# Four fused layers on one core: in the first (retention) layer, |scores| of two quads are added on GpSimd for half of the heads before they are summed on TensorE

## The chip, the core and the metric

One core of a Trainium2 chip. The whole program (four layers, one launch) runs on it, and the metric is the device time of one execution in microseconds. The engines are named as in the profile: PE (TensorE), PEld (its weight loads), ACT (ScalarE), DVE (VectorE), POOL (GpSimd), SP (SyncE, which here only issues DMAs).

## The reference, cut to what matters

The input is 8 images of 32x32 positions and 256 channels. Four layers follow one another, each added to its input. The change touches only the first, a retention layer with 8 heads of 32 channels and L = 1024 tokens:

```python
xf = groupnorm(x).reshape(B, L, E)
q, k, vr = heads(xf @ Wq.T), heads(xf @ Wk.T * SCALING), heads(xf @ Wv.T)
qr, kr = theta_shift(q, sin, cos), theta_shift(k, sin, cos)     # q*cos + rot(q)*sin
qk  = einsum('bhqd,bhkd->bhqk', qr, kr) * mask[None]
den = clip(abs(qk).sum(-1, keepdims=True), 1.0, 50000.0)
out = einsum('bhqk,bhkd->bhqd', qk / den, vr)
out = layernorm_over_head(out) * ln_g + ln_b
out = gelu(out) @ Wo.T
```

So each score is needed twice: as it is (for `out`) and as an absolute value summed over the keys (for `den`).

## The kernel before, in words

**Quads.** `layer0` cuts the work of an image into 32 *quads* (L655 on): for each half `c` of the heads (4 heads), each half `h` of the 1024 queries, and each of 8 blocks `kb` of 128 keys. All 8 images make 256 quads, numbered n. A quad handles 4 heads at once, in two PSUM tiles `s` of 128 x (2 heads x 512 queries); the ring of `s` tiles has 3 places.

**What one quad does.**
- `scores(n)` (L668): for each of the two tiles, two 32-row matmuls on PE (L675; each fp32 matmul is two instructions in the profile, so a quad has eight), then DVE multiplies the tile with the decay mask into SBUF, `e` (L681).
- `absolute(n, i)` (L683): ACT writes `ea = |e|` (L685).
- `sums(n - 2)` (L687): four matmuls with a 128 x 32 block of ones add up `ea` over the keys into the PSUM tile `sm` (L693). This is "a set of sums"; every quad has one, for the quad two before it. After kb = 7, DVE clamps `sm` into `dn` (L701).
- `nums(n - 1)` (L709): four matmuls of `v` with `e` into `num` (L720); after kb = 7 ACT copies it to `nm` (L728).

The loop at the end of `layer0` emits, for each n: scores(n), absolute(n, 0), sums(n-2), nums(n-1), absolute(n, 1), and then the *units* that are due.

**Units.** All other work is cut into units and given to `fill` with the number of a quad, after which it is emitted: `project` (q or k of one half of the tokens: 2 matmuls L550, a DVE shuffle L554 into `sh`, an ACT copy L555 into `xc`; after the second half POOL rotates: L560, L561, L563 for k, and L565, L567 as well for q), `values` (L534, L538), `normed` (POOL writes the normalised image `xn`, L236), `gn.stats/mean/root` (the group norm's statistics on DVE, with two tiny matmuls and a `pow` on POOL, L223), `ahead` (SP loads a coming image), and for each half of the heads the `tail`: POOL makes `sq` = nm*nm + dn*dn*1e-5 (L578, L579, with an ACT Square L576), `var` (L584, then a table load, Ln and Exp on ACT), `norm` (two DVE multiplies of `sq` and `nm`, L591, then a table load and Gelu on ACT), and `output` (L603, a DVE add L608, a store by SP).

**Order.** PE, DVE and ACT run in the order in which `layer0` writes the instructions (`manual_schedule`); on POOL and SP the order is a scheduler's. Each engine runs its queue in order. PE needs `e` from DVE for nums, `ea` from ACT for sums, and a free `s` place for scores and for every unit's PSUM tile (they share the ring).

**Memory.** `x` images and the next layer's first tiles share a ring of three 1 MB buffers, `K.big`; `xn` has its own buffer; `ea` has 4 buffers, `e` 4.

Of the kernel before, what the change touches and what calls it, by code (L numbers as in the profile page):

```python
# [434 lines left out]

class Fillers:


# [20 lines left out]
def layer0(tc, K, src, dst, n_img, a, first):  # L461
    nc = tc.nc
    with tc.tile_pool(name="l0c", bufs=1) as cp, tc.tile_pool(
# [48 lines left out]
        def flat(t):  # L512
            return t.rearrange("p a n -> p (a n)")

        xn, v, qk, hT, nm, dn, turned = ({} for _ in range(7))
        fill = Fillers()

        K.ring = lambda name: pair(name)[:, 0, :]
        gn = GroupNorm(K, n_img)

        def normed(b):
            gn.shift(b)
            xn[b] = wk.tile([P, 2, L], F32, name="xn")
            for c in range(2):
                gn.apply(nc.gpsimd, b, c, xn[b][:, c, :], x[b][:, c, :])

        def values(b, u):
            if u == 0:
# [13 lines left out]
        def project(b, s, c, h):  # L542
            if h == 0:
                turned[0] = wk.tile([P, L], F32, name="sh")
                turned[1] = wk.tile([P, L], F32, name="xc")
            sh, xc = turned[0], turned[1]
            ps = pair("qk_ps")[:, 0]
            hs = slice(h * HALF, (h + 1) * HALF)
            for kc in range(2):
                nc.tensor.matmul(  # L550
                    ps, w[:, s, kc, c * P : (c + 1) * P], xn[b][:, kc, hs],
                    start=kc == 0, stop=kc == 1,
                )
            nc.vector.stream_shuffle(sh[:, hs], ps, [i ^ 1 for i in range(32)])  # L554
            nc.scalar.copy(xc[:, hs], ps)  # L555
            if h == 0:
                return
            d = wk.tile([P, L], F32, name=f"qk{s}{c}")
            qk[b, s, c] = d
            nc.gpsimd.tensor_mul(v3(sh), v3(sh), hankel(63))  # L560
            nc.gpsimd.tensor_mul(v3(xc), v3(xc), hankel(0))  # L561
            if s == 1:
                nc.gpsimd.tensor_add(d, xc, sh)  # L563
            else:
                nc.gpsimd.tensor_add(xc, xc, sh)  # L565
                o = 126 + 32 * c
                nc.gpsimd.tensor_mul(  # L567
                    v3(d), v3(xc), rot[:, o : o + 32].unsqueeze(2).to_broadcast([P, 32, 32])
                )


        def tail(b, c):
            m, d = nm.pop((b, c)), dn.pop((b, c))
            if c == 0:
                hT[b] = wk.tile([P, 2, L], F32, name="hT")
            nc.scalar.activation(d, d, AF.Square, scale=math.sqrt(1e-5))  # L576
            sq = wk.tile([P, L], F32, name="sq")
            nc.gpsimd.tensor_mul(sq, flat(m), flat(m))  # L578
            nc.gpsimd.tensor_add(sq, sq, flat(d))  # L579

            def var():
                ps = pair("var_ps")
                for h, hs in halves():
                    nc.tensor.matmul(ps[:, h], hd[:, 1, :], sq[:, hs], start=True, stop=True)  # L584
                nc.scalar.preload_act_table_set("natural_log_exp_and_others")
                nc.scalar.activation(sq, flat(ps), AF.Ln)
                nc.scalar.activation(sq, sq, AF.Exp, scale=-0.5)

            def norm(h):
                hs = slice(h * HALF, (h + 1) * HALF)  # L590
                nc.vector.tensor_mul(sq[:, hs], m[:, h], sq[:, hs])  # L591
                if h == 1:
                    nc.scalar.activation(
                        hT[b][:, c, :], sq, AF.Gelu, bias=gb[:, 1:2], scale=gb[:, 0:1]
                    )

            return var, norm

        def output(b, m, h):
            ps = pair("o_ps")[:, 0]  # L600
# [13 lines left out]
        def prepare(b):  # L614

            n = 32 * b
            for i in range(4):
                fill.add(
                    n + (0, 1, 3, 4)[i],
                    lambda s=1 - i // 2, h=i % 2: project(b, s, 1, h),  # L620
                )
            if b == 0 and n_img > 1:
                x[1] = load(1)
                measure(1, 6)
            if b + 2 < n_img:
                def ahead():
                    x[b + 2] = load(b + 2)

                fill.add(n + 16, ahead)
                measure(b + 2, n + 23)  # L630
            if b + 1 < n_img:
                fill.add(n + 15, lambda: normed(b + 1))
                for i in range(4):
                    fill.add(
                        n + (17, 18, 20, 21)[i],
                        lambda s=1 - i // 2, h=i % 2: project(b + 1, s, 0, h),
                    )
                    fill.add(n + 23 + i, lambda u=i: values(b + 1, u))

        def measure(b, at):  # L640
            for i in range(4):
                fill.add(at + i, lambda i=i: gn.stats(b, image_parts(x[b]), i))
            fill.add(at + 5, lambda: gn.mean(b))
            fill.add(at + 7, lambda: gn.root(b))

        def follow(nx):
            n = 32 * n_img
            for i, u in enumerate(nx.early()):
                fill.add(2 + i if i else 0, u)
            fill.add(n - 46, nx.load)  # L650
            for i in range(4):
                fill.add(n - 38 + i, lambda i=i: nx.stats(i))
            fill.add(n - 33, nx.mean)
            fill.add(n - 31, nx.root)
            for c in range(2):  # L655
                fill.add(n - 27 + c, lambda c=c: nx.norm(c))
            fill.add(n - 12, nx.weights)

        quads = [
            (b, c, h, kb)  # L660
# [4 lines left out]
        ]  # L665
        e, ea, acc = {}, {}, {}

        def scores(n):  # L668
            b, c, h, kb = quads[n]
            o = (28 - 4 * kb) * 32 + HALF * h  # L670
            for i in range(2):
                s = pair("s")
                for j in (2 * i, 2 * i + 1):
                    g = slice(32 * j, 32 * j + 32)
                    nc.tensor.matmul(  # L675
                        s[:, j % 2], qk[b, 1, c][g, kb * P : (kb + 1) * P],
                        qk[b, 0, c][g, h * HALF : (h + 1) * HALF], start=True, stop=True,
                    )
                e[n, i] = wk.tile([P, 2, HALF], F32, name="e", bufs=4)
                m = mask[:, 4 * c + 2 * i : 4 * c + 2 * i + 2, o : o + HALF]  # L680
                nc.vector.tensor_mul(e[n, i], s, m)  # L681

        def absolute(n, i):  # L683
            ea[n, i] = wk.tile([P, 2, HALF], F32, name="ea", bufs=4)
            nc.scalar.activation(ea[n, i], e[n, i], AF.Abs)  # L685

        def sums(n):  # L687
            b, c, h, kb = quads[n]
            if kb == 0:
                acc["sm"] = pp.tile([P, HALF], F32, tag="sm", name="sm")  # L690
            for j in range(4):
                g = slice(32 * j, 32 * j + 32)
                nc.tensor.matmul(  # L693
                    acc["sm"][g, :], ones, ea[n, j // 2][:, j % 2, :],
                    start=kb == 0, stop=kb == 7,
                )
            del ea[n, 0], ea[n, 1]
            if kb == 7:
                if h == 0:
                    dn[b, c] = wk.tile([P, 2, HALF], F32, name="dn")  # L700
                nc.vector.tensor_scalar(  # L701
                    dn[b, c][:, h], acc["sm"], 1.0, 50000.0, ALU.max, ALU.min
                )
                if h == 1:
                    var, norm = tail(b, c)
                    fill.add(n + 7, var)
                    for h in range(2):
                        fill.add(n + 9 + h, lambda h=h: norm(h))
                    if c == 1:  # L709
                        for i in range(4):  # L710
                            fill.add(n + 12 + i, lambda i=i: output(b, i // 2, i % 2))

        def nums(n):
            b, c, h, kb = quads[n]
# [15 lines left out]
        engines = {mybir.EngineType.PE, mybir.EngineType.DVE, mybir.EngineType.Activation}  # L730
        with tc.manual_schedule(engines=engines):
            gn.stats(0, image_parts(x[0]))
            gn.mean(0)
            gn.root(0)
            normed(0)
            for s in (1, 0):
                for h in range(2):
                    project(0, s, 0, h)
            for u in range(4):
                values(0, u)  # L740
            N = len(quads)
# [2 lines left out]
            for n in range(N + 2):  # L744
                if n % 32 == 0 and n < N:
                    prepare(n // 32)
                if n < N:
                    scores(n)
                    absolute(n, 0)
                if n >= 2:  # L750
                    sums(n - 2)
                if 1 <= n <= N:
                    nums(n - 1)
                if n < N:
# [1608 lines left out]
```

## Time and profile before

| | us |
|---|---|
| time, median of 3 runs | 3330.1 (3329.66 to 3331.37) |
| the profiled execution's own time | 3334.75 |
| its span, first to last instruction | 3333.0 |
| first quad's scores start | 40.0 |
| last quad's scores start | 1060.9 |
| first matmul of the next layer (L843) | 1089.6 |
| PE busy from 100 to 1000, per 100 us | 99.3 to 100.0 |
| DVE, ACT, POOL busy from 100 to 1000, per 100 us | 69 to 73, 66 to 71, 23 to 42 |

The profile is one execution seen by the hardware profiler. A *busy* figure adds up the time in which an engine had an instruction running; *mean ns* is one instruction's duration. PE runs up to four narrow matmuls beside each other, so what a set of matmuls costs is read from the distance between starts in the timeline, not from the duration of one.

### The profile page before, as it was taken

What the parts mean: (1) busy time and instruction counts of PE and PEld (TensorE: products, weight loads), DVE (VectorE), ACT (ScalarE), POOL (GpSimd) and SP (SyncE); (2) the same over time, 40 slices, a digit from 0 to 9 for tenths busy, and PEclk for the clock granted to TensorE, in tenths of its full rate; (3) what the DMA queues carried; (4) which work ended last, traced back from release to release, by engine and by line L of the source; (5) the groups of instructions that cost most, each with busy time, mean ns of one, the idle gap of its engine ahead of it and who ended that gap; (6) DMA issues with size and microseconds to landing.
All of it is one profiled execution on the core that took longest, in us unless ns stands there. A gap on an engine that the chain in (4) does not pass through costs nothing. (4 is left out here: it accounts for less than half of the span.)

```text
span 3333.0 us, 77642 instructions
## 1 busy us (share of the span) xinstructions
PE 3203.6 (96%) x30792; PEld 1649.6 (49%) x30792; DVE 2185.0 (66%) x5570; ACT 2277.6 (68%) x5066; POOL 1491.7 (45%) x1073
## 2 busy tenths in 40 slices
PE   7999999999998999899999999999998999999997
PEld 3323323233232444667677766666664555555554
DVE  4776776777676667565555655666665667777775
ACT  3666666666676457755556547767676779888885
POOL 4233223323431011245444445344335658888777
PEclk9999999999999999999999999999998889999999
DMA  3000000000000666777787731111111001101001
GB/s 141 14 26 1 26 26 1 26 7 20 26 1 32 221 235 238 234 202 191 193 216 200 187 115 58 53 65 40 50 52 36 14 14 38 35 30 36 27 27 61
DMA packets 139183, 268.00 MB, mean 80 GB/s; under 512 B 9218, under 2 KB 77700, under 8 KB 130500
## 3 DMA queue, kind: packets, MB, share of 16 engines
q1 hardware_dynamic: 132436, 242.67, 24.3%
q10 hardware_dynamic: 6384, 20.37, 1.8%
q8 instruction: 243, 3.98, 0.5%
q14 instruction: 120, 0.98, 0.1%
HBM read 177.81 MB, written 85.20 MB: 79 GB/s over the span
## 5 line engine op out<-in xcount | busy, mean ns | idle before, releaser
L681 DVE TENSOR_TENSOR e<-s,ret 128x1024 f32<-128x1024 f32 x512 | 602.9, 1219 | 180.4 <-PE s L675 176.4
L685 ACT ACTIVATE ea<-e 128x1024 f32<-128x1024 f32 x512 | 535.1, 1055 | 267.8 <-DVE e L681 233.9
L675 PE MATMUL s<-qk,qk 32*128 32x512 f32 x2048 | 300.4, 640 | 2.4 <-POOL qk L567 1.7
L1564 POOL TENSOR_TENSOR e<-e,su 128x616 f32<-128x616 f32 (+2 forms) x128 | 157.3, 1229 | 269.8 <-DVE su L1563 240.2
L693 PE MATMUL sm<-ea,ones 128*32 128x512 f32 x2048 | 273.0, 604 | 2.0 <-DVE dn L701 2.0
L720 PE MATMUL num<-e,v 128*32 128x512 f32 x2048 | 266.6, 592 | 0.0
L1711 DVE COPY pts<-pt 112x512 f32<-112x512 f32 x256 | 175.9, 687 | 133.4 <-PE pt L1706 131.7
L2076 ACT ACTIVATE e<-win,disc 128x196 f32<-128x196 f32 x512 | 239.7, 544 | 0.3
L843 PE MATMUL up_ps<-x,wup 128*128 128x512 f32 x512 | 230.7, 605 | 3.2 <-POOL x L236 3.2
L1696 POOL TENSOR_TENSOR e<-e,su 128x784 f32<-128x784 f32 x128 | 191.3, 1495 | 82.7 <-DVE su L1695 53.9
L1688 ACT ACTIVATE e<-e,mx 128x196 f32<-128x196 f32 x512 | 228.0, 454 | 0.0
L2083 POOL TENSOR_TENSOR e<-e,win 128x784 f32<-128x784 f32 x128 | 201.7, 1576 | 37.8 <-issue 31.6
L1559 ACT ACTIVATE e<-e,mx 128x154 f32<-128x154 f32 (+2 forms) x512 | 212.3, 426 | 0.0
L1059 ACT ACTIVATE d<-d,cols 128x128 f32<-128x128 f32 x512 | 163.8, 392 | 67.9 <-POOL d L1050 67.8
L870 DVE SCALAR_TENSOR_TENSOR cv<-xm,par,cv 128x512 f32<-128x512 f32 x192 | 144.7, 754 | 85.5 <-ACT cv L865 80.9
L2015 PE MATMUL qkv_ps<-xq,w 128*128 128x512 f32 x384 | 191.4, 625 | 1.2 <-ACT fac L2110 1.2
L1255 POOL TENSOR_TENSOR decayed<-state,rb 128x520 f32<-128x520 f32 x48 | 50.8, 1058 | 304.7 <-PE sc L1188 112.5
L1796 PE MATMUL qkv_ps<-x,w 128*128 128x512 f32 x384 | 182.7, 613 | 1.6 <-POOL x L236 1.6
L1706 PEld LDWEIGHTS pt<-idg,e 128*112 128x112 f32 x1024 | 120.3, 139 | 120.5 <-issue 90.6
L675 PEld LDWEIGHTS s<-qk,qk 32*128 32x128 f32 x2048 | 85.3, 183 | 184.2 <-issue 120.4
L1706 PE MATMUL pt<-idg,e 128*112 128x128 f32 x1024 | 164.7, 287 | 8.4 <-DVE oT L1730 3.1
L1678 DVE CUSTOM_DVE_ANT_0 e<-s,e 128x196 f32<-128x196 f32 x512 | 153.7, 357 | 8.0 <-PE s L1665 4.2
(244 smaller groups left out, 6775.6 us busy)
## 6 DMA issues: line engine op xcount, KB each, us to landing
d<-l1rows SPq DMA_DIRECT2D x64, 512.0 KB
x<-x SPq DMA_DIRECT2D x25, 1024.0 KB
l1xm<-xm SPq DMA_DIRECT2D x16, 1024.0 KB
l1sz<-sz SPq DMA_DIRECT2D x16, 1024.0 KB
xv<-l1xm SPq DMA_DIRECT2D x32, 512.0 KB
l1xa<-xa SPq DMA_DIRECT2D x16, 1024.0 KB
xa<-l1xa SPq DMA_DIRECT2D x16, 1024.0 KB
rb<-l1rows SPq DMA_DIRECT2D x32, 512.0 KB
```

Of the source, the lines that this page charges most:

```text
L675: nc.tensor.matmul(s[:, j % 2], qk[b, 1, c][g, kb * P : (kb + 1) * P], qk[b, 0, c][g, h * HALF : (h + 1) * HALF], start=True, stop=True,)
L681: nc.vector.tensor_mul(e[n, i], s, m)
L685: nc.scalar.activation(ea[n, i], e[n, i], AF.Abs)
L693: nc.tensor.matmul(acc["sm"][g, :], ones, ea[n, j // 2][:, j % 2, :], start=kb == 0, stop=kb == 7,)
L720: nc.tensor.matmul(acc["num"][g, :], v[b][:, kb, vc], e[n, j // 2][:, j % 2, :], start=kb == 0, stop=kb == 7,)
L843: nc.tensor.matmul(ps, wup[:, kc, m * P : (m + 1) * P], seg(s)[:, kc], start=kc == 0, stop=kc == 1,)
L1559: self.nc.scalar.activation(p[:, j], p[:, j], AF.Exp, scale=-1.0, bias=mx[:, j : j + 1], accum_out=su[:, j : j + 1],)
L1688: self.nc.scalar.activation(e[:, j], e[:, j], AF.Exp, scale=-1.0, bias=mx[:, j : j + 1], accum_out=self.su[:, j : j + 1],)
L1706: self.nc.tensor.transpose(ps[: self.PART, at : at + P], self.tile(n)[:, 2 * i + j, k * self.PART : (k + 1) * self.PART], self.K.ident,)
L2015: nc.tensor.matmul(ps, w[:, kc, o : o + P], xq[b][:, kc, h * HALF : (h + 1) * HALF], start=kc == 0, stop=kc == 1,)
L2076: nc.scalar.activation(e[:, j], win[:, 0], AF.Tanh, scale=disc[b][:, i, 8 + h : 9 + h], bias=disc[b][:, i, h : h + 1],)
L2083: nc.gpsimd.tensor_add(e, e, win[:, 1].unsqueeze(1).to_broadcast([P, 4, NWIN]))
```

## The change

It touches only `layer0`. In words:

1. Quads are taken in groups of four. In the second quad of a group POOL adds the `ea` tile of heads 0 and 1 of the first quad to that of the second; in the fourth quad it adds heads 2 and 3 of the third (for this the third and fourth quad do their two tiles in the other order). So a group's 8 `ea` tiles become 6, and a group has three sets of sums instead of four, in the quads with n mod 4 = 3, 0 and 1. The quads with n mod 4 = 2 have none. `ea` gets 6 buffers.
2. POOL's instructions are put under the written order as well. To that end the rotation becomes units of one POOL instruction each (`rotate`), `normed` is cut in two, and the squares of `nm` become a unit of their own (`squared`); `total` (the Square and the add of `dn`) too.
3. The units get new quads: the PE units mostly those with n mod 4 = 2, and some of the others.
4. `xn` moves into the ring of three 1 MB buffers, and an image is loaded after quad 9 of the image before it (it was after quad 16, one image earlier still); its statistics follow after quads 11 and 12. The next layer's first image is loaded 23 quads before the end and not 46.

```diff
-        def normed(b):
-            gn.shift(b)
-            xn[b] = wk.tile([P, 2, L], F32, name="xn")
-            for c in range(2):
-                gn.apply(nc.gpsimd, b, c, xn[b][:, c, :], x[b][:, c, :])
+        def normed(b, c):
+            if c == 0:
+                gn.shift(b)
+                xn[b] = K.big("xn")
+            gn.apply(nc.gpsimd, b, c, xn[b][:, c, :], x[b][:, c, :])
...
+            heads(b, 1, n, n + 2, n + 3, n + 7, n + 8, n + 9)
+            if b + 1 < n_img:
...
+                fill.add(n + 9, ahead)
...
+                        n + 11 + i // 2,
+                        lambda i=i: gn.stats(b + 1, image_parts(x[b + 1]), i),
...
+                fill.add(n + 13, lambda: gn.mean(b + 1))
+                fill.add(n + 14, lambda: gn.root(b + 1))
+                for c in range(2):
+                    fill.add(n + 16 + c, lambda c=c: normed(b + 1, c))
+                heads(b + 1, 0, n + 18, n + 19, n + 20, n + 24, n + 25, n + 26)
+                for i in range(4):
+                    fill.add(n + (21, 26, 28, 30)[i], lambda u=i: values(b + 1, u))
...
+        def order(n):
+
+            return (0, 1) if n % 4 < 2 else (1, 0)
...
-        def absolute(n, i):
-            ea[n, i] = wk.tile([P, 2, HALF], F32, name="ea", bufs=4)
+        def absolute(n, k):
+
+
+            i = order(n)[k]
+            ea[n, i] = wk.tile([P, 2, HALF], F32, name="ea", bufs=6)
             nc.scalar.activation(ea[n, i], e[n, i], AF.Abs)
-
-        def sums(n):
+            if n % 2 and k == 0:
+                nc.gpsimd.tensor_add(ea[n, i], ea[n, i], ea.pop((n - 1, i)))
+
+        def sums(n, k):
+
             b, c, h, kb = quads[n]
-            if kb == 0:
+            if kb == 0 and k == 0:
                 acc["sm"] = pp.tile([P, HALF], F32, tag="sm", name="sm")
+            two = [ea.pop((n + (1, 2, 3)[k], 0)), ea.pop((n + (0, 1, 3)[k], 1))]
             for j in range(4):
                 g = slice(32 * j, 32 * j + 32)
                 nc.tensor.matmul(
-                    acc["sm"][g, :], ones, ea[n, j // 2][:, j % 2, :],
-                    start=kb == 0, stop=kb == 7,
-                )
...
-                    var, norm = tail(b, c)
-                    fill.add(n + 7, var)
+                    total, var, norm = tail(b, c)
+                    fill.add(n + 6, total)
+                    fill.add(n + 10, var)
                     for h in range(2):
-                        fill.add(n + 9 + h, lambda h=h: norm(h))
+                        fill.add(n + 11 + h, lambda h=h: norm(h))
                     if c == 1:
                         for i in range(4):
-                            fill.add(n + 12 + i, lambda i=i: output(b, i // 2, i % 2))
+                            fill.add(n + (14, 15, 17, 18)[i], lambda i=i: output(b, i // 2, i % 2))
...
-        with tc.manual_schedule(engines=engines):
+        with tc.manual_schedule(engines={E.PE, E.Activation, E.DVE, E.Pool}):
...
-                if n >= 2:
-                    sums(n - 2)
+                if n % 4 == 3:
+                    sums(n - 3, 0)
+                elif n % 4 < 2 and n > 1:
+                    sums(n // 4 * 4 - 4, n % 4 + 1)
```

In `sums` and what follows it, n is now the group's first quad, so the `tail` units fall on the quads 2 (total), 6 (var), 7 and 8 (norm) and 10, 11, 13, 14 (output) of the next image for c = 1, and on 18, 22, 23 and 24 of the same image for c = 0. The instruction listing of the changed program has 64 sets of sums fewer on PE, 128 adds more on POOL, and the same instructions in the same order on all engines from the next layer on.

More of the change, by code (lines that the diff above doesn't have):

```diff
@@ L513, in flat @@
             return t.rearrange("p a n -> p (a n)")
-        xn, v, qk, hT, nm, dn, turned = ({} for _ in range(7))
+        xn, v, qk, hT, nm, dn, sqs, turned = ({} for _ in range(8))
         fill = Fillers()
@@ L555, in project, with rotate, squared, total @@
             nc.scalar.copy(xc[:, hs], ps)
[L556 to L563, printed above, removed]
+        def rotate(b, s, c, i):
+            sh, xc = turned[0], turned[1]
+            if i == 0:
+                qk[b, s, c] = wk.tile([P, L], F32, name=f"qk{s}{c}")
+                nc.gpsimd.tensor_mul(v3(sh), v3(sh), hankel(63))
+            elif i == 1:
+                nc.gpsimd.tensor_mul(v3(xc), v3(xc), hankel(0))
+            elif i == 2:
+                nc.gpsimd.tensor_add(qk[b, s, c] if s else xc, xc, sh)
             else:
-                nc.gpsimd.tensor_add(xc, xc, sh)
                 o = 126 + 32 * c
                 nc.gpsimd.tensor_mul(
-                    v3(d), v3(xc), rot[:, o : o + 32].unsqueeze(2).to_broadcast([P, 32, 32])
-                )
+                    v3(qk[b, s, c]), v3(xc),
+                    rot[:, o : o + 32].unsqueeze(2).to_broadcast([P, 32, 32]),
+                )
+        def squared(b, c):
+            sqs[b, c] = wk.tile([P, L], F32, name="sq")
+            m = flat(nm[b, c])
+            nc.gpsimd.tensor_mul(sqs[b, c], m, m)
         def tail(b, c):
-            m, d = nm.pop((b, c)), dn.pop((b, c))
+            m, d, sq = nm.pop((b, c)), dn.pop((b, c)), sqs.pop((b, c))
             if c == 0:
                 hT[b] = wk.tile([P, 2, L], F32, name="hT")
[L576 to L579, printed above, removed]
+            def total():
+                nc.scalar.activation(d, d, AF.Square, scale=math.sqrt(1e-5))
+                nc.gpsimd.tensor_add(sq, sq, flat(d))
             def var():
@@ L595, in norm @@
                     )
-            return var, norm
+            return total, var, norm
         def output(b, m, h):
@@ L616, in prepare, with heads @@
             n = 32 * b
[L617 to L620, printed above, removed]
-                )
[L622 to L625, printed above, removed]
-                def ahead():
[L627 to L632, printed above, removed]
+            def heads(b, c, k0, k1, k, q0, q1, q):
+                for s, h, at in ((1, 0, k0), (1, 1, k1), (0, 0, q0), (0, 1, q1)):
+                    fill.add(at, lambda s=s, h=h: project(b, s, c, h))
+                for s, at in ((1, k), (0, q)):
+                    for i in range(4 - s):
+                        fill.add(at + i, lambda s=s, i=i: rotate(b, s, c, i))
+            heads(b, 1, n, n + 2, n + 3, n + 7, n + 8, n + 9)
+            if b + 1 < n_img:
+                def ahead():
+                    x[b + 1] = load(b + 1)
+                fill.add(n + 9, ahead)
                 for i in range(4):
                     fill.add(
-                        n + (17, 18, 20, 21)[i],
-                        lambda s=1 - i // 2, h=i % 2: project(b + 1, s, 0, h),
-                    )
[L638 to L644, printed above, removed]
+                        n + 11 + i // 2,
+                        lambda i=i: gn.stats(b + 1, image_parts(x[b + 1]), i),
+                    )
+                fill.add(n + 13, lambda: gn.mean(b + 1))
[5 more added lines that the diff above has]
+                    fill.add(n + (21, 26, 28, 30)[i], lambda u=i: values(b + 1, u))
         def follow(nx):
@@ L649, in follow @@
                 fill.add(2 + i if i else 0, u)
-            fill.add(n - 46, nx.load)
+            fill.add(n - 23, nx.load)
             for i in range(4):
-                fill.add(n - 38 + i, lambda i=i: nx.stats(i))
-            fill.add(n - 33, nx.mean)
-            fill.add(n - 31, nx.root)
+                fill.add(n - 19 + i, lambda i=i: nx.stats(i))
+            fill.add(n - 14, nx.mean)
+            fill.add(n - 12, nx.root)
             for c in range(2):
-                fill.add(n - 27 + c, lambda c=c: nx.norm(c))
-            fill.add(n - 12, nx.weights)
+                fill.add(n - 9 + c, lambda c=c: nx.norm(c))
+            fill.add(n - 13, nx.weights)
         quads = [
@@ L670, in scores @@
             o = (28 - 4 * kb) * 32 + HALF * h
-            for i in range(2):
+            for i in order(n):
                 s = pair("s")
@@ L693, in sums @@
                 nc.tensor.matmul(
-                    acc["sm"][g, :], ones, ea[n, j // 2][:, j % 2, :],
-                    start=kb == 0, stop=kb == 7,
-                )
-            del ea[n, 0], ea[n, 1]
-            if kb == 7:
+                    acc["sm"][g, :], ones, two[j // 2][:, j % 2, :],
+                    start=kb == 0 and k == 0, stop=kb == 4 and k == 2,
+                )
+            if kb == 4 and k == 2:
                 if h == 0:
@@ L728, in nums @@
                 nc.scalar.copy(nm[b, c][:, h], acc["num"])
-        engines = {mybir.EngineType.PE, mybir.EngineType.DVE, mybir.EngineType.Activation}
-        with tc.manual_schedule(engines=engines):
+                if h == 1:
+                    fill.add(n + 1, lambda: squared(b, c))
+        E = mybir.EngineType
+        with tc.manual_schedule(engines={E.PE, E.Activation, E.DVE, E.Pool}):
             gn.stats(0, image_parts(x[0]))
@@ L734, in layer0 @@
             gn.root(0)
-            normed(0)
+            for c in range(2):
+                normed(0, c)
             for s in (1, 0):
@@ L738, in layer0 @@
                     project(0, s, 0, h)
+                for i in range(4 - s):
+                    rotate(0, s, 0, i)
             for u in range(4):
```

## The prediction, made before the changed kernel was run

> **What bounds the kernel now.** First I read the engines' busy shares by stretches of 100 us, because the shares of the whole span (PE 96%, POOL 45%) mix four layers. Columns: stretch, its length, then PE, PEld, DVE, ACT, POOL busy with counts, granted clock, DMA share, GB/s.
>
> ```profile
> 500.00:600.00 100.00, 99.32 (x664) 31.34 (x666) 70.24 (x84) 69.76 (x75) 38.17 (x18) 1.00 0.00 1
> 600.00:700.00 100.00, 100.00 (x656) 31.72 (x648) 70.60 (x83) 65.92 (x70) 24.93 (x14) 1.00 0.06 22
> ```
>
> The reader is to see that in the changed layer PE never rests, at full clock, DMA is nearly idle and POOL has 60 to 75% free. A PE that is always busy can still be waiting inside its pipeline, so next comes the timeline of one plain quad (start, duration, engine).
>
> ```profile
> 331.90 1.14 PE L675 MATMUL s<-qk,qk 32*128 32x512 f32 x8
> ...
> 332.97 1.07 PE L693 MATMUL sm<-ea,ones 128*32 128x512 f32 x8
> 333.14 2.36 DVE L681 TENSOR_TENSOR e<-s,ret 128x1024 f32<-128x1024 f32 x2 [0.57 <-PE s L675]
> ...
> 333.85 1.04 PE L720 MATMUL num<-e,v 128*32 128x512 f32 x8
> ...
> 334.46 1.06 ACT L685 ACTIVATE ea<-e 128x1024 f32<-128x1024 f32 x1 [0.25 <-DVE e L681]
> ...
> 334.82 1.14 PE L675 MATMUL s<-qk,qk 32*128 32x512 f32 x8
> ```
>
> Starts: scores 331.90, sums 332.97, nums 333.85, next scores 334.82. So scores hold PE for 1.07, **a set of sums for 0.88**, nums for 0.97; a quad is 2.92. DVE needs 2.36 of it, ACT about 2.1. A quad with a PE unit (four matmul rows) is 4.84, so a unit is 1.92. One image of the middle lasts 130.35 (first scores at 298.36 and at 428.72): 32 x 2.92 = 93.4, 18 units x 1.92 = 34.6 and two tiny group-norm products of 0.31 make 128.6; the other 1.75 are stalls: 0.57 after the q projection (DVE's shuffle waits for POOL's k rotation to free `sh`), 0.26 at quad 10, two of 0.41 behind the group-norm products.
>
> **The change, part by part.**
>
> *Removed:* 8 sets of sums per image, 64 in all. Over 100 to 1060 us, 1896 rows of L693 take 209.17 us from start to start, so a set of eight costs 0.882. 64 x 0.882 = **56.5 us**, all on the path, since PE is the bound.
>
> *Added:* 16 POOL adds per image. The nearest rows are POOL's adds of the same size:
>
> ```profile
> L563 POOL TENSOR_TENSOR qk<-xc,sh 128x1024 f32<-128x1024 f32 x16 | 37.8, 2363 | 1.2
> L579 POOL TENSOR_TENSOR sq<-sq,dn 128x1024 f32<-128x1024 f32 x16 | 38.2, 2386 | 44.8 <-ACT dn L576 44.8
> ```
>
> 2.38 us each, 38 us per image. POOL's other work per image is 8 x 2.21 + 4 x 2.38 (the rotations' muls and adds) + 2 x 1.92 + 2 x (1.89 + 2.39) + 2 x 1.20 = 42 (sizes from the groups L560 to L567, L578, L579, L236), so it is busy for 80 of about 124 us. There is room; what counts is lateness, because each add is a new wait of PE. Timing one: the group's second tile product ends 1.25 + 1.18 after its quad's start, Abs 1.06 and about 0.15 of handover each: 3.65; add 2.38: done at about 6.2. The adds of the second quad are needed two quads later, at 2.92 + (2.04 + 1.92) + 1.07 = 7.95: 1.7 to spare. Those of the fourth feed the second half of a set, at 2.92 + 2.92 + 1.07 + 0.44 = 7.35: 1.1 to spare. Where POOL has other work queued ahead this goes:
> - quad 3: the tail's `total` runs ahead of it until 5.2 after quad 3's start (Square behind the shuffle and copy of quad 2's projection), the add ends at 7.6: PE waits 0.35.
> - quad 5: two rotation muls (4.4) stand between that add and this one: PE waits 0.45.
> - Elsewhere the rotations end before the next Abs. Behind the add in POOL's queue stand only rotations, `xn` and `sq`, each needed quads later; the latest, q's last mul in quad 29, ends 1.7 before quad 32 reads it.
>
> *Quads without sums* last 2.04 on PE, less than DVE's 2.36. In images 0 to 6 each has a PE unit (3.96), which hides that. In the last image those at 18, 26 and 30 have none; the next quad's sums then come 1.92 earlier, 0.3 before the add is done: 3 x 0.3. At the very end the last set waits about 1.1 for its add, since no more scores stand before it. Together 2.
>
> *Moved units.* `var` at 22 and its Ln (table 1.28, Ln 1.03) free their PSUM place 0.4 after quad 24's scores want it, with one unit fewer between: 0.4 per image. The k-to-q stall (0.57) goes, as five quads now lie between those projections. The group-norm stalls (0.8) stay. Loads: a 1 MB load was issued at 233.42 and its packets ended 6.3 later; it is now issued at quad 9's start and first read by DVE at about 10.5 after, so 4 us are spare, where they were some 27. The store of the old image has some 3 us before `xn` takes its buffer. I cost both at nothing; if that cover went, DVE or POOL would stand still and PE with it, microsecond for microsecond, 7 times.
>
> *DVE against POOL.* A wait of this kind is in the trace: the DVE operation below, with both inputs in SBUF, takes 0.22 with POOL idle, and when a POOL `tensor_tensor` is running, as long as that takes to end.
>
> ```profile
> L2061 DVE SCALAR_TENSOR_TENSOR disc<-dth,disc x16: 224/666/1447, 2535.1 to 3177.7; 128x64 f32<-128x64 f32 x16
> L591 DVE TENSOR_TENSOR sq<-nm,sq x32: 636/681/692, 141.8 to 1077.8; 128x512 f32<-128x512 f32 x32
> ```
>
> (min/median/max ns.) Of the layer's operations, only the norm multiply L591 is of this form and size, and before it never met POOL (0.64 to 0.69). The mask product, one input in PSUM, doesn't care: 136 of them wholly under POOL have a median of 1.224, 312 clear of it 1.216. With POOL busy for 80 of 124, an L591 can lose 0 to 2.4. Placing them: the first of quad 7 falls into that quad's add and loses 1.7; the others fall into gaps. DVE is then late into quads 8 and 9, and PE waits about 0.75 (a PSUM place and `e`). The Trainium skill, "SBUF — State Buffer", section "Who interferes with whom", has the rule for this: a DVE instruction with two SBUF inputs and a GpSimd instruction that reads SBUF exclude each other for the whole instruction. It speaks against this change: by the rule without placement, 32 multiplies that each meet a whole add lose 32 x 2.4 = 77 us, more than the sums give back; by the trace's placement one in four is met.
>
> *Sum per image:* new stalls 0.35 + 0.45 + 0.4 + 0.75 + 0.1 = 2.05, old ones gone 0.57 + 0.26 = 0.83: 1.2 lost in 7 images, 8.4, and 2 at the end: about 10. 56.5 - 10 = **46 us gained**. The profiled execution took 3334.75 (span 3333.0 and 1.75 around it), so it would take 3288.5; the median of the runs shown lies 4.65 below the profiled one, at 3330.1, so I forecast 3330.1 - 46 = **3284**. Later layers issue the same instructions, so nothing is added there. Own range: all new stalls absent and old ones gone, 56.5 + 7 x 0.83 = 62, would be 3268; twice the stalls, 36, 3294.
>
> **The rivals.**
> 1. *DVE takes over where sums are missing.* If the units don't hide it, a set gives back 2.92 - 2.36 = 0.56 and not 0.88: 64 x 0.56 = 36, less 10: **3304**. For: 2.36 > 2.04, and units put DVE work there too. Against: DVE per image is 32 x 2.36 + some 20 = 96 of 124, and three PSUM places let it lag.
> 2. *Slower: POOL's queue sets the pace.* In order, six adds per image stand right behind rotation work of up to 4.4. If each were late by all of it beyond its spare 1.65, 6 x 2.75 x 8 = 132 would be lost against 56: **3406**. It outweighs the gain from 56.5 / 48 = 1.2 us of lateness on each of them. For: two of the adds are late by my own count. Against: POOL is free for 44 of 124, and most rotations end before the next Abs does.
> 3. *The gain is given back exactly* (half of rival 2, or loads late by some 6 us beyond their spare 4, 7 times): **3330**. Against: the loads moved their 1 MB in 5.0 and 3.6 us.
>
> That the change doesn't do what it says is excluded: the listing has 64 sets fewer and 128 adds more.
>
> **How the numbers follow.** Forecast case 0.75; rival 1, 0.15; rival 3, 0.03; rival 2 and the like, 0.07. About 0.2% (7 us) is what a measurement here can tell from no change. Faster: 0.75 + 0.15 = 0.90; same 0.03; slower 0.07. The range takes the forecast's own and rival 1 with some of its stalls: 3269 to 3308, leaving out rivals 2 and 3 and a little on each side.
>
> **What would show it.** Right: in the middle of the layer, images of 123 to 125 us, groups of four quads with three sets of 0.88, PE still above 98% busy, L591 with one in four stretched to about 2.3, POOL adds of 2.4. PE waits for POOL's `ea` of about 0.8 per image, in quads 5 and 7 alone. The last scores start near 1015. Rival 1: PE idle, or L675 waiting for L681, in quads with n mod 4 = 2 or 3. Rival 2: waits of L693 for POOL over 1 us, spread over the image. I am wrong if bn_stats waits for the DMA, if the mask product gets longer than 1.23, or if PE's clock falls below 1.00 in the layer.

## The result, and the profile after

The medians on one chip: 3302.89 us for the changed kernel (3299.98 to 3305.22, 4 runs) against 3330.73 for the kernel before (4 runs): ratio **0.9911, 95% interval [0.9899, 0.9923]**. The forecast was 3284.0 with a range of 3269 to 3308. So the change makes the kernel faster, but by 28 us where 46 were forecast. The profiled executions give 3334.75 and 3305.0, a gain of 29.8 of those 46; the working below is made against these two, since their traces can be laid beside each other.

The busy shares by stretches of 100 us, of the changed kernel, with the columns as before:

```profile
500.00:600.00 100.00, 99.72 (x642) 31.36 (x635) 75.52 (x84) 72.09 (x76) 63.49 (x29) 1.00 0.05 17
600.00:700.00 100.00, 98.38 (x649) 29.83 (x648) 70.74 (x76) 71.89 (x76) 64.22 (x30) 1.00 0.02 6
```

POOL, which was busy for 25 and 38% of these stretches, is busy for 64% now. PE, which had 99.3 and 100.0, has lost 1.6 in the second stretch: there is a gap in it now. The clock is still 1.00. The timeline of PE in the fourth image, a quad with sums and one without:

```profile
466.29 1.14 PE L688 MATMUL s<-qk,qk 32*128 32x512 f32 x8
467.37 1.06 PE L713 MATMUL sm<-ea,ones 128*32 128x512 f32 x8
468.25 1.04 PE L740 MATMUL num<-e,v 128*32 128x512 f32 x8
...
471.82 1.14 PE L688 MATMUL s<-qk,qk 32*128 32x512 f32 x8
472.89 1.07 PE L740 MATMUL num<-e,v 128*32 128x512 f32 x8
```

From 467.37 to 468.25 the set of sums holds PE for 0.88; in the quad of 471.82 the numerators follow the scores directly, and the 0.88 is gone. The groups on the page say the same by their counts:

```profile
L703 POOL TENSOR_TENSOR ea<-ea 128x1024 f32<-128x1024 f32 x128 | 304.1, 2376 | 284.9 <-ACT ea L701 216.9
L713 PE MATMUL sm<-ea,ones 128*32 128x512 f32 x1536 | 208.8, 604 | 1.6 <-POOL ea L703 1.6
```

128 adds of 2.376 us (forecast 2.38), and 1536 rows of sums, that is 192 sets of eight where 256 were. Note the last column: it says that PE itself stood idle only 1.6 us for these adds. Waits inside a set don't show in it: in quad 5 of the third image the set lasts 1.46 where others last 1.06, since its second half waits for an add. The waits of PE between 100 and 1030 us show what it did stand idle for (in all, times, longest):

```profile
PE qk_ps L552 <- POOL xn L236: 9.9, 7, 1.5
PE sm L713 <- POOL ea L703: 1.4, 1, 1.4
PE s L688 <- DVE e L694: 0.7, 1, 0.7
```

Seven waits of 1.4 on average, one per image, for the normalised image `xn`. The prediction has no such wait.

Where the 29.8 came from, by the starts of scores in the two traces:

| stretch | before | after | gained | forecast |
|---|---|---|---|---|
| start to first scores | 40.0 | 40.7 | -0.7 | 0 |
| image 0 | 128.0 | 125.7 | 2.3 | 5.9 |
| images 1 to 6 | 781.0 | 750.2 | 30.8 | 35.2 |
| image 7 and the end, to L843 (after: L870) | 140.6 | 140.6 | 0.0 | 5.1 |
| later layers | 2243.4 | 2246.0 | -2.7 | 0 |

(Forecast: 8 x 0.882 - 1.2 = 5.86 per image for seven images, and 7.06 - 2 for the last.) The later layers issue the same instructions in all kernels here, and took from 2238.6 to 2250.4 us in the profiles. The granted clock falls to 0.5 there for stretches of 3 to 24 us, which add up to 139 us in the shortest of them (`xn` before the add) and to 178 in the longest (`total` later). So edits of a few us are read below from the first layer's traces first, and from the medians second.

A middle image (images 1, 2 and 4) lasts 124.96, inside the 123 to 125 that the prediction named, and the last scores start at 1025.8 where it said about 1015.

### The profile page after: what moved, and what is told of

Read it like the earlier page. It is cut to its first block, busy times and chain, and to the rows that moved or that the text cites. A ratio compares the mean times of both kernels' runs of the same rounds, so it can differ in the third digit from the quotient of the medians.

```text
span 3303.2 us, 76346 instructions
## 1 busy us (share of the span) xinstructions
PE 3165.7 (96%) x30280; PEld 1638.2 (50%) x30280; DVE 2192.5 (66%) x5570; ACT 2278.5 (69%) x5066; POOL 1792.1 (54%) x1201
## 5 line engine op out<-in xcount | busy, mean ns | idle before, releaser
L703 POOL TENSOR_TENSOR ea<-ea 128x1024 f32<-128x1024 f32 x128 | 304.1, 2376 | 284.9 <-ACT ea L701 216.9
L870 PE MATMUL up_ps<-x,wup 128*128 128x512 f32 x512 | 230.2, 604 | 4.0 <-POOL x L236 3.2
L2110 POOL TENSOR_TENSOR e<-e,win 128x784 f32<-128x784 f32 x128 | 201.7, 1576 | 38.5 <-issue 31.6
L713 PE MATMUL sm<-ea,ones 128*32 128x512 f32 x1536 | 208.8, 604 | 1.6 <-POOL ea L703 1.6
```

What stands on the lines that cost most here:

```text
L703: nc.gpsimd.tensor_add(ea[n, i], ea[n, i], ea.pop((n - 1, i)))
L870: nc.tensor.matmul(ps, wup[:, kc, m * P : (m + 1) * P], seg(s)[:, kc], start=kc == 0, stop=kc == 1,)
```

## The experiments

**Theory.** The gain per removed set is as forecast (0.88), and the adds give some of it back in four places: the second half of `xn`, which stands behind an add in POOL's queue and is needed at once; the first quads, where the next layer's early units wait for POOL; a rotation ahead of an add (quad 5) and a DVE multiply under one (quad 7); and the last image. **Rivals:** the sets give back less than 0.88 because DVE takes over; the moved units, not the adds, lose the time; a GpSimd add is the wrong place, DVE would do it in half the time.

Traces beside medians, all in us ("image" is the third, "to next" runs from the last scores to the next layer's first matmul):

| run | median | ratio to before, interval | image 0 | image | image 7 | to next | next layer at |
|---|---|---|---|---|---|---|---|
| before | 3330.7 | | 128.0 | 130.35 | 111.9 | 28.7 | 1089.6 |
| after | 3302.9 | 0.9911 [0.9899, 0.9923] | 125.7 | 124.96 | 109.2 | 31.4 | 1057.2 |
| places only | 3333.8 | 0.9997 [0.9986, 1.0008] | 128.1 | 129.51 | 112.3 | 29.5 | 1086.9 |
| no POOL adds | 3274.7 | 0.9826 [0.9812, 0.9840] | 121.8 | 122.37 | 107.2 | 29.0 | 1031.9 |
| adds on DVE | 3398.3 | 1.0197 [1.0182, 1.0212] | 133.0 | 137.01 | 128.1 | 30.7 | 1155.9 |
| `xn` before the add | 3289.9 | 0.9871 [0.9852, 0.9890] | 125.0 | 123.28 | 109.2 | 31.0 | 1044.0 |
| and early units moved | 3286.7 | 0.9858 [0.9840, 0.9875] | 120.3 | 123.30 | 110.8 | 30.3 | 1041.0 |
| and four sets at the end | 3293.9 | 0.9873 [0.9853, 0.9892] | 127.6 | 123.28 | 109.3 | 29.1 | 1045.6 |
| and `total` later | 3290.2 | 0.9865 [0.9843, 0.9887] | 127.4 | 122.90 | 108.8 | 31.6 | 1045.2 |
| and both norms in one quad | 3293.4 | 0.9874 [0.9851, 0.9898] | 126.8 | 123.32 | 109.1 | 30.6 | 1046.7 |
| `xn` and the next three | **3282.4** | **0.9839 [0.9822, 0.9855]** | 119.8 | 122.91 | 108.9 | 28.1 | 1034.3 |
| those and both norms | 3286.8 | 0.9852 [0.9830, 0.9874] | 120.2 | 122.93 | 109.3 | 29.3 | 1035.6 |

Each "and" is `xn` before the add with that one edit. The kernels ran on different chips, on which the kernel before took from 3330.7 to 3336.3, so ratios are compared, not medians. Single traces also differ where no edit reaches: the first scores start at 38.8 to 40.7 in them, and image 0, which has the same instructions in the runs "`xn` before the add" and "four sets at the end", took 125.0 and 127.6. So in the last column some 3 us are chance.

### `xn` before the add

```diff
-                    fill.add(n + 16 + c, lambda c=c: normed(b + 1, c))
+                    fill.add(n + 15 + c, lambda c=c: normed(b + 1, c))
```

> The changed kernel with one edit: the two units that write the normalised image (normed) come after quads 15 and 16 instead of 16 and 17, so that the second no longer stands behind the add of quad 17 in GpSimd's queue. Theory (queue order): quad 18 of images 0 to 6, which lasts 5.66 us where 3.98 was due, goes back to about 4.0, since its projection waited 1.4 to 1.7 us for xn alone; 7 x 1.68 = 11.8 us less, so about 3291. Rival (another wait is as late): the projection then waits for something else of the same lateness, such as the store that frees xn's buffer, and quad 18 stays above 5 us: 3300 or more.

Measured: 0.9871, and a middle image of 123.28, 1.68 less, in every one of images 1 to 6. First the place in the changed kernel's timeline:

```profile
486.02 2.38 POOL L703 TENSOR_TENSOR ea<-ea 128x1024 f32<-128x1024 f32 x1
487.10 1.12 PE L552 MATMUL qk_ps<-xn,w 128*128 128x512 f32 x2
488.38 1.21 POOL L236 TENSOR_SCALAR xn<-x,gn 128x1024 f32<-128x1024 f32 x1
489.64 1.13 PE L552 MATMUL qk_ps<-xn,w 128*128 128x512 f32 x2 [1.41 <-POOL xn L236]
```

POOL starts quad 17's add at 486.02; the second half of `xn` (due in the same quad) waits for it until 488.38 and ends at 489.59. PE starts the first two matmuls of the projection, which read the first half, at 487.10, and cannot go on before 489.64. The same place with the edit, in that run's timeline:

```profile
476.31 2.38 POOL L236 TENSOR_SCALAR xn<-x,gn 128x1024 f32<-128x1024 f32 x2
...
480.51 2.38 POOL L703 TENSOR_TENSOR ea<-ea 128x1024 f32<-128x1024 f32 x1
...
481.09 1.98 PE L552 MATMUL qk_ps<-xn,w 128*128 128x512 f32 x4
```

Both halves are done by 478.69, and the projection's four matmuls run in one piece while the add is still running. Quad 18 goes from 5.66 to 3.98, and no other quad of a middle image changes. Seven images, 7 x 1.68 = 11.8: this is what the one-line edit brings (11.2 in the trace, from the first scores to the next layer), and it is the largest single loss of the change.

### No POOL adds, and places only

```diff
-                nc.gpsimd.tensor_add(ea[n, i], ea[n, i], ea.pop((n - 1, i)))
+                ea.pop((n - 1, i))
```

> The changed kernel without the 128 adds on GpSimd; the three sets of sums per group stay, so the scores of one quad of each pair are left out of the divisor for that half of the heads. It shows what the adds cost by keeping GpSimd's queue busy. Theory (queue order): all stalls that come from adds go: in a middle image 0.38 at quad 5, 0.18 at quad 7, 0.54 at quad 9, 1.68 at quad 18, together about 2.8 of the image's 124.96, 20 us in 7 images, and some 5 more in the first and the last image: about 3278. The norm multiply of quad 7 is no longer stretched (2.2 us to 0.69). Rival (the adds' own lateness is small and the rest of the missing gain is paid by the new places of the units): 3293 or more, with quad 18 still above 5 us.

This kernel leaves the scores of every other quad out of the divisor for half of the heads; it shows only what the adds cost. The second run has the new places and the written order of POOL, but four sets and no adds:

```diff
-                if n % 4 == 3:
-                    sums(n - 3, 0)
-                elif n % 4 < 2 and n > 1:
-                    sums(n // 4 * 4 - 4, n % 4 + 1)
+                if n >= 2:
+                    sums(n - 2)
```

> The changed kernel with all new places of units, the written order on GpSimd, the new buffers and loads, but with a set of sums in every quad again and no adds. Theory (the removed sets are the whole gain): the 56.5 us of the 64 sets come back on top of what the kernel without adds takes, so 3278 + 56 = about 3334, the kernel before within 5 us. Rival (the new places are a good part of the gain): 3322 or less.

Measured: 0.9826 and 0.9997. The three traces between them price the parts of the change, to the next layer's first matmul. The moved units: 1089.6 to 1086.9, 2.7 gained (by the times 0.9997, no difference). The 64 sets: 1086.9 to 1031.9, **55.0 gained** (forecast 56.5), and 129.51 - 122.37 = 7.14 per image, 8 x 0.89. The adds: 1031.9 to 1057.2, **25.3 given back** (1.4 of it before the first scores, where there is no add yet).

So the first rival falls for every quad that has a PE unit: a set gives its whole 0.88 and not 0.56, and quads without sums last 3.98 where 2.04 + 1.92 = 3.96 was expected. In the last image, three quads without sums have no unit, and there the rival is right twice: quads 18 to 21 last 13.21 without adds and 13.22 with four sets, quads 24 to 27 12.36 and 12.07, so the sets missing in quads 18 and 26 give nothing, adds or no adds (quad 30's gives its 0.86). That is about the 1.5 by which 55.0 falls short of 56.5. On the whole the moved units by themselves lose nothing; the loss comes with the adds.

Of it, 124.96 - 122.37 = 2.6 lies in each middle image: quad 18 (1.68), quad 9 (0.54) and quad 5 (0.38). Their sum is 2.60.

### The adds on DVE

```diff
-                nc.gpsimd.tensor_add(ea[n, i], ea[n, i], ea.pop((n - 1, i)))
+                nc.vector.tensor_add(ea[n, i], ea[n, i], ea.pop((n - 1, i)))
```

> The changed kernel with the 128 adds on VectorE instead of GpSimd. The 512-wide multiply with both inputs in SBUF takes 0.69, so a 1024-wide add is some 1.25 us, 20 us per image on an engine that has 96 of 125 busy. Theory (VectorE has little left and runs in order): the waits behind adds on GpSimd go, but each add stands before the next mask product, and a group of four then needs 4 x 2.36 + 2 x 1.25 = 11.9 on VectorE against 3 x 2.92 + 2.04 = 10.8 on TensorE where no unit gives time: about 3305 to 3320. Rival (an add is half as long there and takes no lock, so it is the better place): 3295 or less.

Measured: 1.0197, slower than the kernel before and far beyond what was expected of it. The Trainium skill, "GPSIMD Engine Reference", section "3.1 Elementwise — side-by-side cycle accounting", gives for an fp32 add of 2048 elements 2.29 us on DVE and 4.50 on GpSimd, a ratio of 1.96; here, at 1024, GpSimd takes 2.38 and DVE, where POOL is idle, 1.23: the page agrees with the rows. By durations alone the adds belong on DVE. The timeline of this run shows why they do not:

```profile
470.39 2.36 POOL L568 TENSOR_TENSOR qk<-xc,sh 128x1024 f32<-128x1024 f32 x1
470.60 3.23 DVE L703 TENSOR_TENSOR ea<-ea 128x1024 f32<-128x1024 f32 x1
...
473.75 4.87 DVE L694 TENSOR_TENSOR e<-s,ret 128x1024 f32<-128x1024 f32 x4
475.02 2.26 PE L688 MATMUL s<-qk,qk 32*128 32x512 f32 x8 [0.79 <-DVE e L694]
```

The add starts at 470.60, 0.21 after a POOL rotation, and ends at 473.83; the rotation ends at 472.75, so 1.08 of the add lay after that. Four mask products stand behind it, and PE's scores, whose PSUM places these free, wait. The group of all 128 adds:

```profile
L703 DVE TENSOR_TENSOR ea<-ea 128x1024 f32<-128x1024 f32 x128 | 219.1, 1712 | 75.7 <-ACT ea L701 74.1
```

A mean of 1.71, and 74 us of waiting for ACT's `ea` just ahead of them, in a queue that PE needs for every quad. 16 adds cost DVE 16 x 1.71 = 27 and 74 / 8 = 9 of waiting per image; DVE had 96 of 124 to do. 132 is more than the image was long, and it became 137. The granted clock, 1.00 in all other runs between 200 and 1000 us, was 0.99 here, which can be a part of the other 5.

### The early units of the next layer

On top of `xn` before the add, the next layer's 13 early units (small products of its weights, and the POOL operations that feed them) go to quads where POOL has room:

```diff
-                fill.add(2 + i if i else 0, u)
+                fill.add((0, 4, 6, 6, 6, 10, 10, 8, 11, 11, 12, 14, 14)[i], u)
```

> xn_before_add, and in the first image the 13 early units of the next layer moved: their products come after quads 6, 10, 11 and 14 instead of 4, 7, 10 and 13, with the copies out of PSUM in the same quad and the GpSimd multiplies ahead of them where its queue is shorter. Theory (in the first image PE waits for GpSimd's multiplies behind the rotations, and projections wait for a PSUM place that a copy of a later quad frees): the first image, 124.96 us in xn_before_add, loses about 1.1 at quad 4, 0.5 at 7, 1.6 at 8, 2.0 at 10, 1.6 at 11: 118.5 us, and the next layer's first matmul starts near 1038 instead of 1044.0. Rival (the first image pays for DMAs or for its own group norm): 123 us or more.

Image 0 in the changed kernel and in this run, one of these products (L322) in each timeline:

```profile
84.03 0.49 PE L322 MATMUL prep_ps<-prep 128*128 128x128 f32 x2 [1.72 <-POOL prep L314]
```

```profile
78.12 0.49 PE L322 MATMUL prep_ps<-prep 128*128 128x128 f32 x2
```

Before the edit the POOL operations that this product reads (L314) stand behind an add (80.88 to 83.25), which itself had waited for its inputs, and PE stands idle for 1.72. After it PE does not wait here. Image 0 lasts 120.3, 119.8 and 120.2 in the three runs with this edit, and 125.0 to 127.6 in the four that have `xn` before the add without it: 5 to 8 us, once. Not all of this was lost to the adds: quad 4 lasts 5.28 with adds and 4.14 without, but quad 8 lasts 6.43 in both and in "places only" too, and 4.84 after this edit, so its 1.6 came with the new places or the written order of POOL. Image 7 of this run is 1.65 longer than without the edit, which does not reach it: in its quads 27 and 28 the granted clock is 0.66 on average from 999 to 1004 us.

### Four sets in the last image's uncovered groups

```diff
+        def four(n):
+            return n // 4 * 4 - 32 * n_img in (-16, -8, -4)
...
-            if n % 2 and k == 0:
+            if n % 2 and k == 0 and not four(n):
```

(and `sums` and the loop accordingly)

> xn_before_add, and in three groups of the last image (its quads 16 to 19 and 24 to 31) no adds and four sets again. Theory (where no unit fills the quad without sums, the next set stands 1.9 us closer to its add and PE waits; a set is then worth less than the wait): the groups that last 2.92 + 2.92 + 2.60 + 4.04 = 12.5 and 2.92 + 3.42 + 2.07 + 4.99 = 13.4 go to 11.7 each, and the last set no longer waits for its add: the next layer's first matmul 3 to 4 us earlier, near 1040.5. Rival (the waits there are for Gelu and the masks, and adds pay everywhere): no earlier than 1043.5.

An uncovered group is one whose quad without sums has no PE unit. In the changed kernel the longest wait of the last image is this one, in its timeline:

```profile
1013.58 2.37 POOL L703 TENSOR_TENSOR ea<-ea 128x1024 f32<-128x1024 f32 x1 [1.88 <-ACT ea L701]
...
1016.00 1.06 PE L713 MATMUL sm<-ea,ones 128*32 128x512 f32 x8 [1.38 <-POOL ea L703]
```

ACT is late with `ea` (a table load and Gelu of the first half run there), so is the add, and no unit stands before the sums: 1.38 idle. With four sets the stretch from the last scores to the next layer falls from 31.0 to 29.1, but image 7 stays at 109.3 (109.2): quads 19 and 27, where PE had waited, are shorter by 3.1, and quads 18, 26 and 30, which have their sums again, longer by 3.25. The gain is 1.8 us in the trace where 3 to 4 were expected, and the medians cannot show it (0.9873 against 0.9871). The next layer starts at 1045.6, which is past the bound that the expectation set for its rival (1043.5); but the start and image 0, which this edit does not reach, are 3.4 longer here than in `xn` before the add, so that bound decides nothing.

### `total` later

```diff
-            heads(b, 1, n, n + 2, n + 3, n + 7, n + 8, n + 9)
+            heads(b, 1, n, n + 2, n + 4, n + 7, n + 8, n + 9)
...
-                    fill.add(n + 6, total)
+                    fill.add(n + 7, total)
```

> xn_before_add, with the unit total one quad later (behind the add of quad 3 instead of ahead of it) and k's rotation one quad later. Theory (quad 5's 0.38 is the add of quad 3 behind total in GpSimd's queue): quad 5 goes from 3.31 to 2.93 in images 1 to 7, 2.6 us in all, if the later rotation does not make a new wait at quad 7's shuffle: the next layer's first matmul near 1041.5. Rival (the later rotation only moves the wait to quads 7 and 8, whose projection needs the buffer that it frees): as many us come back there, 1044 or later.

Quad 5 goes from 3.31 to 2.93 and a middle image from 123.28 to 122.90: the 0.38 was POOL's work between the adds, `total` and rotations, near the forecast (0.45). The 5.02 and 4.84 of quads 7 and 8 stay, so the wait did not move there, as the rival has it. (That the next layer starts at 1045.2 and not at 1041.5 is mostly the start and image 0: 3.3 longer than in `xn` before the add.) The edit moves `total` and a rotation together, so it does not tell which of them made the 0.38. Seven times 0.38 is 2.7, under what the medians can tell here: 0.9865 [0.9843, 0.9887] against 0.9871 [0.9852, 0.9890]. The trace shows it, the times do not.

### Both norm multiplies in one quad

The 0.54 of quad 9 was left. In the changed kernel, DVE's first norm multiply (L601) and what follows, in the timeline:

```profile
446.40 2.37 POOL L703 TENSOR_TENSOR ea<-ea 128x1024 f32<-128x1024 f32 x1 [2.02 <-ACT ea L701]
...
447.11 2.21 DVE L601 TENSOR_TENSOR sq<-nm,sq 128x512 f32<-128x512 f32 x1
449.24 2.34 DVE L694 TENSOR_TENSOR e<-s,ret 128x1024 f32<-128x1024 f32 x2
451.09 1.67 PE L688 MATMUL s<-qk,qk 32*128 32x512 f32 x8
```

The add holds from 446.40 to 448.77; the multiply, issued at 447.11, ends at 449.32, 0.55 after the add. Without an add it takes 0.68. The mask products behind it are 1.5 late, and quad 9's scores take 1.67 and not 1.14: their second tile waits for its PSUM place. The edit puts the multiply into quad 8, where no add runs:

```diff
-                        fill.add(n + 11 + h, lambda h=h: norm(h))
+                        fill.add(n + 12, lambda h=h: norm(h))
```

> The normed image ahead of the add, as in the run with that edit, and the first norm multiply one quad later (quads 8 and 24 instead of 7 and 23), where no POOL add stands in the way. Theory (the multiply of quad 7 is held by POOL's add, 2.22 instead of 0.69, which makes DVE's mask products of quad 8 late, and quad 9's second scores tile waits for its PSUM place): no L601 over 0.75 us in the middle images, quad 9 goes from 3.46 to 2.92, an image from 123.29 to about 122.75, 7 x 0.54 = 3.8 us: about 3286 where the run without this edit had 3289.9. Rival (the 0.54 is the add's own lateness for the sums of quad 9, the multiply is only near it): the multiply becomes short all the same, quad 9 stays at 3.46, time unchanged. Second rival (two multiplies and a shuffle in one quad are too much for DVE): quad 9 or 10 keeps 0.3 to 0.6.

> The same edit of the norm multiply on top of the four edits that gave 3282.35 together. Theory: 7 x 0.54 = 3.8 us less, about 3278.6, middle image 122.90 to about 122.36, last scores from 1006.2 to about 1002.5. Rival: unchanged, 3282.

Measured: the multiplies are short, but an image stays at 123.32 (123.28), and with the other edits at 122.93 (122.91). The timeline of the first of the two runs at the same place:

```profile
448.92 1.27 DVE L601 TENSOR_TENSOR sq<-nm,sq 128x512 f32<-128x512 f32 x2
450.11 2.35 DVE L694 TENSOR_TENSOR e<-s,ret 128x1024 f32<-128x1024 f32 x2
451.10 1.41 PE L688 MATMUL s<-qk,qk 32*128 32x512 f32 x8
```

Quad 9 is 2.92, as the theory says: the 0.54 was the add's hold on DVE, and the first rival (the add's own lateness) falls. But two multiplies and a shuffle in one quad are too much for DVE, as the second rival says: 1.41 is quad 10's scores, still waiting, and quads 10 and 26 are longer by 0.33 and 0.24. Together 0.57 comes back for the 0.54. So the mechanism is shown, and this way round it brings nothing. A place that has neither an add nor the other multiply was not tried.

### The three edits together

> The edits of xn_before_add, early_moved, last_four_sets and total_later together. If each is a wait of its own, they add up: 5.5 + 3.5 + 2.6 us off xn_before_add, the next layer's first matmul near 1032.5 and the time near 3278, about what the kernel with no adds at all takes. If they are one backlog in GpSimd's queue seen in several places, less than two thirds of that: 1037 or later.

Measured: 3282.35, ratio **0.9839 [0.9822, 0.9855]**, the fastest of the kernels that compute the whole layer: better than the kernel before by 1.6%, and by its interval better than the changed kernel. The theory expected the next layer at 1032.5 and 3278 us, the rival 1037 or later: with 1034.3, 9.8 of the expected 11.6 us came, so most of these waits do add up. Its busy shares:

```profile
500.00:600.00 100.00, 99.82 (x648) 30.46 (x644) 78.35 (x90) 70.90 (x75) 65.12 (x31) 1.00 0.06 22
600.00:700.00 100.00, 99.79 (x646) 30.78 (x648) 73.55 (x80) 74.06 (x79) 63.25 (x29) 1.00 0.04 13
```

PE has no gap left, with POOL as busy as before. Without any adds the next layer would start at 1031.9 (the run that leaves them out); here it starts at 1034.3. That is 22.9 earlier than in the changed kernel, against the 25.3 that the adds had cost there; all but the last image's three sets and their adds is the work of moved units.

## Why the prediction was right and wrong

The direction and the mechanism held: PE bounds the layer, 64 sets go, and nearly every one is worth its whole distance from start to start. The size was not right. The forecast gave its own case 62 to 36 us of gain, 3268 to 3294; the measured 3302.9 lies outside that, and inside 3269 to 3308 only because the range was widened for rival 1, which is not what happened: that part is luck. The 36 itself was reckoned wrong: it is twice the net loss, while twice the new stalls would be 2 x 2.05 - 0.83 = 3.27 in each of seven images and 4 at the end, 27 in all, and leave a gain of about 30, which is near what the profiles have.

In the profiles the gain was short by 16: 0.7 at the start, 3.6 in image 0, 4.4 in images 1 to 6, 5.0 in image 7 and the end, and 2.7 in later layers, which is no effect of the change.

**The removed sets:** 55.0 for 56.5. Right, but for two sets of the last image that gave nothing.

**The step that failed:** "Behind the add in POOL's queue stand only rotations, `xn` and `sq`, each needed quads later". The second half of `xn` is due in quad 17, behind that quad's add, and is read by the projection in quad 18, one quad later and not quads later. The add's lateness was worked out against the work ahead of it, and the work behind it only in a sentence. It cost 1.68 per image, 11.8 in all, and one line undoes it.

**Why a middle image was nearly right all the same** (124.96, forecast 130.35 - 5.86 = 124.5): the missed 1.68 was made up for by costs that were put too high or that did not come. Per image:

| step | forecast | measured |
|---|---|---|
| quad 3, `total` ahead of the add | 0.35 | 0 |
| quad 5, rotations ahead of the add | 0.45 | 0.38 |
| `var` and Ln, a PSUM place | 0.4, quad 24 | 0.18 each in quads 7 and 23 |
| a norm multiply held by the add | 0.75 | 0.54 |
| old stalls that stay (1.75 - 0.83) | 0.92 | about 0.2, in quads 13 and 14 |
| `xn` behind the add | none | 1.68 |

(The 0.1 that the sum also held for smaller things is left out. The 0.18 each are there without adds as well.) With that 0.1 the rows add up to 2.97 forecast and 3.16 measured, and eight quads of 3.98 for 3.96 add 0.16: most of the 0.46 between the images. A sum that agrees does not show that its terms do.

**DVE against POOL:** the placing was right: nearly one multiply in four (7 of 32) stretched, to 2.22 where about 2.3 was forecast, and one more, which met the end of an add in image 7, to 1.06; in this view of the tile (min/median/max ns):

```profile
L601 DVE TENSOR_TENSOR sq<-nm,sq x32: 667/691/2225, 136.2 to 1044.1; 128x512 f32<-128x512 f32 x32
```

The rule of the Trainium skill that the prediction weighed ("SBUF — State Buffer", section "Who interferes with whom") holds in the form that it was used: a wait to the end of the other engine's instruction, and not a mere slowing. The adds on DVE show it best: all 52 that were issued while a POOL operation ran ended 1.08 to 1.09 us after it, whether the two had overlapped for 0.26 us or for 2.29.

**Image 0** was taken to be like the others. It also holds the next layer's early units, whose POOL work now runs in a fixed order between adds and rotations: 5 us, which the run that moves them gives back (1.6 of it, in quad 8, is lost without adds too). With the 1.7 of quad 18 that is more than the 3.6 that are missing; in this trace quad 0 is 1.5 shorter than before (2.98 for 4.45), which it is in only some of the traces. That the order of POOL's queue is written by hand in the changed kernel was read, but what else is in that queue in image 0 was not listed.

**Image 7 and the end:** 2 was forecast. The trace has the quads 18, 26 and 30 as said, but the sums of quad 27 wait 1.38, not 0.3, since ACT runs late there; the last set's lateness and the tail behind it cost 2.7 and not 1.1 (31.4 against 28.7), and the first half of image 7 has the stalls of quads 5, 7 and 9 like the images before it, which were counted for seven images and not eight. These make 1.1 + 1.6 + 1.1 = 3.8 of the 5.0 that are missing there. The set missing in quad 18 gave nothing, with adds or without, where 0.3 was allowed for: 0.6 more. The last 0.6 is not settled.

**The rivals:** the first (DVE takes over) is refuted by the quads of 3.98, and right only for two quads without a unit in the last image, so that the measured time lies near its 3304 for another reason; the second (POOL's queue sets the pace) named the right queue, but the waits are three places and not all over the image; the third did not occur, and no bn_stats waited for a load.

## What to carry to other kernels

When work goes to an engine with time to spare, list what stands *behind* each new instruction in that engine's queue and when each is needed, also in the first and last rounds, where other work is queued; the busy share (64%) says nothing of it. The adds cost 25 us in the first placing; moving units around them, with three sets put back, won 23 us. And an engine that does an operation in half the time can be the wrong place for it, if the operation then waits, in order, ahead of what the bound engine needs.

## What the runs showed of the hardware

A DVE add with both inputs in SBUF took 1.23 us alone and 3.23 when it was issued 0.21 after a POOL operation of 2.36, and ended 1.08 after that operation; the norm multiply took 0.68 and 2.21. The hold goes both ways: in the run with the adds on DVE, POOL's `xn` (L236), 1.20 us in the others, has a mean of 1.68 and reaches 2.17 where an add runs. The mask product, with one input in PSUM, did not care: 1.218 mean with POOL's adds, 1.218 without, between 100 and 1000 us.
